# A recurrent layer between attention layers: where its own-token products, roots and softmax scaling are computed

## The chip, the cores and the metric

The kernel runs on one core of a Trainium2 chip. The metric is device time in microseconds (us), lower is better. All data are 32-bit floats. The engines are named as in the profile: PE is TensorE (matmuls; PEld are its weight loads), DVE is VectorE, ACT is ScalarE, POOL is GpSimd, and SP only issues transfers.

## What is computed

Four layers on x (8 sequences, 100 tokens, 512 channels) with a context of 361 tokens: grouped attention, a recurrent layer, a small attention, and a pair of attentions with an MLP. The change lies in the second and third:

```python
# second layer, per head of 16 channels (32 heads), tokens l in order
w = jnp.exp(-jnp.exp(time_decay + jnp.tanh(xw @ decay_w1) @ decay_w2))
r, k, v = xr @ Wr.T, xk @ Wk.T, xv @ Wv.T
g = jax.nn.silu(xg @ Wg.T)
def step(s, inp):
    k_l, v_l, w_l, r_l = inp
    a = k_l[..., :, None] * v_l[..., None, :]
    out = einsum('bhs,bhst->bht', r_l, faaaa * a + s)   # faaaa * a: the token's own part
    return a + w_l[..., None] * s, out
y = (y - mean(y)) * rsqrt(var(y) + 1e-5) * gn_w + gn_b  # mean and variance per head
x = x + (y * g) @ Wo.T
x = x + sigmoid(xr2 @ fWr.T) * (square(relu(xk2 @ fWk.T)) @ fWv.T)   # channel mix
# third layer
probs = softmax((x @ w_q.T) @ (ctx @ w_k.T).T / sqrt(512))
x = x + alpha * ((probs @ (ctx @ w_v.T)) @ w_o.T)
```

The own-token part of `out` is v times the sum over a head's 16 channels of r * faaaa * k.

## The kernel before

The second layer works in four units of two sequences (`UB = 2`, so 200 token columns, `UT`). Channels lie on the 128 partitions in four chunks c, so a tensor of one unit is [128, 4, 200]; w, k and v have an extra leading column per sequence. There are three kinds of work.

**Preparation** (`prescan`, lines 608 to 712), one generator for each unit: normalization, token shift, the mixes w, k, v, r, g, then the projections v, k, r (`through`, line 598: two halves of two chunks, each half in one PSUM bank and then evicted), the decay w (`pw`, lines 694 to 708), and g. v is also written to DRAM with 16 transfers (line 687), and read back spread over partitions (`spread_values`, line 721). It has 21 turns (a `yield` ends a turn).

**The scan loop** (lines 997 to 1043), 64 steps of 16 per unit: one step is one chunk c and one i of four. `to_psum` (730) copies the spread values to PSUM on ACT. `states` (738) multiplies them by k (line 743, DVE), scans over the tokens (line 745, DVE) and multiplies by r (line 751, POOL). `gather_heads` (754) sums on PE, a step later, into the bank `py`. In steps 2 and 10 of a unit, `own_token` (line 760) forms the own-token part of two chunks: r * faaaa * k on DVE from SBUF (line 766, tile `ruk`), a matmul that sums over the head and spreads over the channels of v (line 770, bank `pu`), and the product with v into y (line 771).

**What follows the scan**: `head_norms` (775) for each half of a unit adds `py` to y (779), subtracts the mean (784), squares (786), sums the squares (791), and takes the root (793, ACT) into two of the four row groups of `sd`. `after` (795) inverts the roots (797), spreads them over the channels (803), applies gn_w, gn_b and g (805, 808), projects, and does the channel mix (lines 823 to 844); for units 1 to 3 its last act is `turned_rows` (846), which transposes x and adds the mix on eviction (line 858). `mixing` (871) is the third layer: for unit 0 it turns its own rows and then ends a turn (886 to 888), then queries (890), scores, softmax (898 to 903), and the rest.

**What sets the order.** All PE instructions are issued in program order (`L1_ORDERED`); the other engines' instructions are ordered by the program's scheduler, which uses its own estimates. In each scan step `advance` (line 945) gives every running generator one turn, or more or fewer by its rate: 1.6 for the preparation of unit 1, 1.1 for later ones, 1.0, 1.2, 1.4 and 1.0 for what follows units 0 to 3. The preparation of unit 0 runs ahead of the loop. Whatever is left when the 64 steps are over runs behind the loop, units by turns.

**Buffers.** Nearly all matmul results of this layer use one tag of three PSUM banks (`bank`, line 540). v, k, r, y and w have two buffers each, so unit u + 2 takes those of unit u; `sd` has one. A buffer is given to the next tile when every instruction on the former one is done. The third layer's tiles of units 1 and 3 take buffers of v and k (`pair_of_tiles`, line 867). The mixes of a preparation have five buffers.

Of the kernel before, what the change touches and what calls it, by code (L numbers as in the profile page):

```python
# [10 lines left out]
F32 = mybir.dt.float32  # L11
AF = mybir.ActivationFunctionType
ALU = mybir.AluOpType
# [3 lines left out]
P = 128  # L17
B, L, C, S = 8, 100, 512, 361
# [38 lines left out]
def kernel(ctx: ExitStack, tc: tile.TileContext, d: dict, out: bass.AP):  # L57
    nc = tc.nc
# [11 lines left out]
    eps5 = const.tile([P, 1], F32, tag="eps5", name="eps5")  # L70
# [5 lines left out]
    def col(name, c):  # L76
        at = PV_AT[name] + c
        return pv[:, at : at + 1]
# [123 lines left out]
    with ExitStack() as es:  # L202
# [15 lines left out]
        v = p1.tile([KB, B, 3, 8 * HV + 16], F32, tag="v", name="v")  # L218
# [292 lines left out]
    with ExitStack() as es:  # L511
# [31 lines left out]
        def two(t):  # L543

            return t[:, : 2 * UT].rearrange("p (c t) -> p c t", c=2)
# [4 lines left out]
        def split(t):  # L550
            return t.rearrange("p c (b l) -> p c b l", l=L)
# [46 lines left out]
        def through(w, m, evict_to):  # L598

            for h in range(2):  # L600
                pp = bank("pp")
                for i in range(2):
                    c = 2 * h + i
                    mm_sum(two(pp)[:, i], [(w[:, k, c * P : (c + 1) * P], m[:, k]) for k in range(NC)])
                evict_to(slice(2 * h, 2 * h + 2), two(pp))
                yield

        def prescan(u, out):
# [81 lines left out]
                            )  # L690
            r = pb.tile([P, NC, UT], F32, tag="r", name="r")
            out["r"] = r
            yield from through(wts["r"], mixes["r"], lambda cs, pp: nc.scalar.copy(r[:, cs], pp))
            for h in range(2):
                pw = bank("pw")
                for i in range(2):
                    c = 2 * h + i
                    nc.tensor.matmul(
                        two(pw)[:, i], lhsT=dw2[:, c * P : (c + 1) * P], rhs=dt, start=True, stop=True
                    )  # L700
                for i in range(2):
                    c = 2 * h + i
                    nc.scalar.activation(
                        two(pw)[:, i], two(pw)[:, i], AF.Exp, bias=col("L1_xattn_time_decay", c), scale=1.0
                    )
                nc.scalar.activation(
                    wT[:, 2 * h : 2 * h + 2, :, 1:], split(two(pw)), AF.Exp, scale=-1.0
                )
                yield
            g = pb.tile([P, NC, UT], F32, tag="g", name="g", bufs=2)  # L710
            out["g"] = g
# [45 lines left out]
                    py[32 * q : 32 * q + 32].rearrange("p (b l) -> p b l", l=L), lhsT=gather[:, i], rhs=st[:, q], start=(i == 0), stop=(i == 3)  # L757
                )

        def own_token(u, c):  # L760

            k, r, v, y = (ready[u][j] for j in "krvy")
            pu = bank("pu")
            for i in range(2):
                ruk = pb.tile([P, UT], F32, tag="ruk", name="ruk")
                nc.vector.scalar_tensor_tensor(
                    ruk.rearrange("p (b l) -> p b l", l=L), r[:, c + i].rearrange("p (b l) -> p b l", l=L),
                    col("L1_xattn_faaaa", c + i), k[:, c + i, :, 1:], ALU.mult, ALU.mult,
                )
                nc.tensor.matmul(two(pu)[:, i], lhsT=heads[:, 0], rhs=ruk, start=True, stop=True)  # L770
            nc.vector.tensor_tensor(
                split(y[:, c : c + 2]), split(two(pu)), v[:, c : c + 2, :, 1:], ALU.mult
            )

        def head_norms(u, c, py):

            y, sd = ready[u]["y"], ready[u]["sd"]
            cs = slice(c, c + 2)
            nc.vector.tensor_tensor(y[:, cs], two(py), y[:, cs], ALU.add)
            yield  # L780
            pg = bank("pg")
            for i in range(2):
                nc.tensor.matmul(two(pg)[:, i], lhsT=heads[:, 1], rhs=y[:, c + i], start=True, stop=True)
            nc.vector.tensor_tensor(y[:, cs], y[:, cs], two(pg), ALU.subtract)
            sq = pb.tile([P, 2, UT], F32, tag="sq", name="sq", bufs=1)
            nc.scalar.activation(sq, y[:, cs], AF.Square)
            yield
            pvar = bank("pvar")
            for i in range(2):
                at = 32 * (c + i)  # L790
                nc.tensor.matmul(pvar[at : at + 32, :UT], lhsT=pick8, rhs=sq[:, i], start=True, stop=True)
            rows = slice(32 * c, 32 * c + 64)
            nc.scalar.activation(sd[rows], pvar[rows, :UT], AF.Sqrt, bias=eps5[rows], scale=1.0)

        def after(u, turned=None, rest=None):
            y, g, sd = (ready[u][j] for j in ("y", "g", "sd"))
            nc.vector.reciprocal(sd, sd)
            yield
            for c0 in (0, 2):
                pair = [bank("rs") for _ in range(2)]  # L800
                for c, rs in zip((c0, c0 + 1), pair):
                    qs = slice(32 * c, 32 * c + 32)
                    nc.tensor.matmul(rs[:, :UT], lhsT=heads[qs, 2], rhs=sd[qs], start=True, stop=True)
                for c, rs in zip((c0, c0 + 1), pair):
                    nc.vector.scalar_tensor_tensor(
                        y[:, c], y[:, c], col("L1_xattn_gn_w", c), rs[:, :UT], ALU.mult, ALU.mult
                    )
                    nc.vector.scalar_tensor_tensor(
                        y[:, c], y[:, c], col("L1_xattn_gn_b", c), g[:, c], ALU.add, ALU.mult
                    )  # L810
                yield
            bs = range(u * UB, (u + 1) * UB)
            for i, b in enumerate(bs):
                po = bank("po")
                mm_sum(po[:L, :], [(y[:, c, i * L : (i + 1) * L], wo1[:, c, :]) for c in range(NC)])
                nc.vector.tensor_tensor(x[b], po[:L, :], x[b], ALU.add)
                stats(pb, b)
                yield
            cols = slice(u * UB, (u + 1) * UB)
            nc.scalar.activation(rstd[:, cols], mv[:, cols, 1], AF.Sqrt, bias=eps5[:L], scale=1.0)  # L820
            nc.vector.reciprocal(rstd[:, cols], rstd[:, cols])
            yield
            got = []
            yield from normed(u, mv, rstd, "L1_xattn_ln2_w", "L1_xattn_ln2_b", got, 0)
            xu = got[0]
            sx = shifted(u, xu, 0)
            yield

            xk, xr, kk = y, sx, xu
            mixed_by(xk, sx, xu, "L1_xattn_fmaa_k")  # L830
            mixed_by(xr, sx, xu, "L1_xattn_fmaa_r")
            yield
            yield from through(wfk, xk, lambda cs, pp: nc.scalar.activation(kk[:, cs], pp, AF.Relu))
            nc.gpsimd.tensor_tensor(kk, kk, kk, ALU.mult)

            yield from through(wfr, xr, lambda cs, pp: nc.scalar.activation(xk[:, cs], pp, AF.Sigmoid))
            yield from through(wfv, kk, lambda cs, pp: nc.vector.tensor_tensor(xk[:, cs], pp, xk[:, cs], ALU.mult))
            if turned is not None:
                tiles = turned()
                tiles.extend(pair_of_tiles((("r", L), ("w", L1)) if u % 2 == 0 else (("v", L1), ("k", L1))))  # L840
                turned_rows(bs, tiles[0], xk)
                rest.append(lambda: added_rows(bs, xk))
            else:
                added_rows(bs, xk)
# [26 lines left out]
        def mixing(u, pool, wqk, wvo, xT, qk, rest=()):  # L871
# [13 lines left out]
                loaded.append((cx, cr))  # L885
            if not rest:
                turned_rows(bs, xT)
                yield
            scale = 1.0 / float(np.sqrt(np.float32(C)))
            yield from through(wqk, xT, lambda cs, pp: nc.scalar.activation(qk[:, cs], pp, AF.Copy, scale=scale))  # L890
            for add in rest:
# [2 lines left out]
            for i, b in enumerate(bs):  # L894
                sc = bank("sc")
                mm_sum(sc[:L, :S], [(qk[:, c, i * L : (i + 1) * L], loaded[i][0][:, c, :]) for c in range(NC)])
                nm = pool.tile([L, 1], F32, tag="nm", name="nm")
                nc.vector.tensor_reduce(nm, sc[:L, :S], AX.X, ALU.max, negate=True)
                pr = pool.tile([L, S], F32, tag="pr", name="pr")
                ss = pool.tile([L, 1], F32, tag="ss", name="ss")  # L900
                nc.scalar.activation(pr, sc[:L, :S], AF.Exp, bias=nm, scale=1.0, accum_out=ss)
                nc.vector.reciprocal(ss, ss)
                nc.vector.tensor_scalar(pr, pr, ss, None, ALU.mult)
                probs.append(pr)
                yield

# [78 lines left out]
        with tc.manual_schedule(engines=L1_ORDERED):  # L985
# [11 lines left out]
            for n in range(NU * STEPS + 1):  # L997
                u, c, i = n // STEPS, n % STEPS // 4, n % 4
                if u < NU:
# [16 lines left out]
                    if n + 1 < NU * STEPS:  # L1016
                        m = n + 1
                        a = to_psum(m // STEPS, m % STEPS // 4, m % 4, va.pop(0))
                    if n % (STEPS // 2) == 2:
                        own_token(u, c)  # L1020
                advance()
                if late is not None:
                    lu, lc, li, lst = late
# [758 lines left out]
```

## Time and profile before

| What | us |
| --- | --- |
| Runs shown: median (lowest to highest of 3) | 2722.99 (2721.82 to 2725.64) |
| Profiled execution: span from the first to the last instruction | 2722.8 |
| PE busy in the span | 2609.8 |
| Scan loop of the second layer, from about 365 to 745 | 380 |
| the rest of the second and third layers behind the loop, to about 829 | 84 |
| DVE busy in the stretch from 365 to 745 | 282.9 |
| ACT busy in the same stretch | 167.9 |

The profile gives no time around its span; span and median agree within 0.2 us. The page has, besides busy times, a line for each engine with the busy share in 40 slices of 68 us each. Other views of the same trace group the instructions by line, engine and tile; list who waited for whom (an engine's idle time ahead of an instruction is put down to the instruction that ended it); follow back the chain of waits; and show the instructions in order of time, where a bracket behind an instruction holds the idle time ahead of it and who ended it. Two PE instructions in the trace make one matmul of 32-bit floats. A duration in the groups and rows is in ns, a start in us from the span's beginning.

### The profile page before, as it was taken

How to read it: one execution, taken by the hardware profiler on the slowest of the kernel's cores; microseconds unless marked ns; L12 is line 12 of the kernel's file. 1: busy time of each engine (PE TensorE's matmuls, PEld its weight loads, DVE VectorE, ACT ScalarE, POOL GpSimd, SP SyncE). 2: the span in 40 equal slices, each digit the busy share in tenths (PEclk: the TensorE clock that was granted, in tenths of full speed). 3: DMA queues.
4: the chain of work that ended last, by engine and by line, in shares of the span. 5: the costliest groups of instructions: out<-in, count | busy, mean ns of one | idle time of the engine just before them, and what ended most of it. 6: DMA issues, size and time to landing. Idle time of an engine off the chain costs nothing.

```text
span 2722.8 us, 39771 instructions
## 1 busy us (share of the span) xinstructions
PE 2609.8 (96%) x14100; PEld 2059.3 (76%) x14100; DVE 1601.2 (59%) x3987; ACT 939.2 (34%) x2143; POOL 1042.7 (38%) x1362
## 2 busy tenths in 40 slices
PE   8999889898989999999999999999999999999999
PEld 5666466676666888877789878788877788887688
DVE  4888366877524556556556556565555655654733
ACT  5777334543321333320333320243331143331211
POOL 2000144433204345455345446344446434535201
PEclk9999888999999999999999999999999999999999
DMA  7432334354214100046200034400015510005400
GB/s 230 119 104 75 115 116 124 92 145 122 81 39 151 55 23 23 4 126 169 80 23 23 1 85 145 136 16 31 12 35 151 150 43 23 23 7 168 152 13 13
DMA packets 149679, 220.58 MB, mean 81 GB/s; under 512 B 45302, under 2 KB 78646, under 8 KB 149226
## 3 DMA queue, kind: packets, MB, share of 16 engines
q1 hardware_dynamic: 149482, 218.05, 27.3%
q8 instruction: 112, 1.84, 0.3%
q14 instruction: 85, 0.70, 0.1%
HBM read 207.48 MB, written 10.53 MB: 80 GB/s over the span
## 4 chain that ended last, share of the span: by engine, by line
PE 67%; POOL 4%; DVE 3%; DMA 2%; ACT 1%; issue 1%; SPq 0%; DVEq 0%; POOLq 0%; ACTq 0%
PE pz L97 16%; PE sl L97 9%; PE pk L1175 6%; PE su L97 6%; PE pq L97 5%; PE pa L97 5%; PE po L1439 5%; PE pp L97 3%; PE pu L97 3%; PE pt L1363 2%; PE pl L97 2%; PE pl L1262 1%; DMA xin<-xd 1%; PE sc L1401 1%; PE sc L97 1%
## 5 line engine op out<-in xcount | busy, mean ns | idle before, releaser
L97 PE MATMUL pz<-at,cr 121*128 121x256 f32 (+1 forms) x960 | 255.9, 378 | 0.0
L751 POOL TENSOR_TENSOR st<-st,r 128x800 f32<-128x800 f32 x64 | 111.9, 1749 | 232.9 <-DVE st L745 198.9
L1336 DVE TENSOR_TENSOR qz<-pz,qz 128x512 f32<-128x512 f32 x192 | 131.9, 687 | 114.0 <-PE pz L97 105.8
L97 PEld LDWEIGHTS pz<-at,cr 121*128 121x128 f32 (+1 forms) x960 | 177.2, 189 | 20.8
L1175 PE MATMUL pk<-q,wb 128*128 128x400 f32 x512 | 190.2, 501 | 0.0
L97 PE MATMUL pa<-qz,wa 128*128 128x400 f32 x512 | 178.7, 500 | 0.8 <-DVE aT L1479 0.8
L97 PE MATMUL sl<-ts,ss 128*128 128x181 f32 x768 | 156.7, 326 | 3.8 <-POOL ts L1231 0.5
L97 PE MATMUL pz<-at,cs 121*128 121x256 f32 (+1 forms) x576 | 149.7, 380 | 0.0
L1248 POOL TENSOR_TENSOR ss<-qz 128x256 f32<-128x256 f32 x96 | 69.8, 727 | 203.3 <-PE su L97 115.0
L97 PEld LDWEIGHTS pa<-qz,wa 128*128 128x128 f32 x512 | 95.7, 190 | 65.9 <-DVE aT L1479 2.3
L1382 ACT ACTIVATE pr<-su,nm 128x362 f32<-128x362 f32 x96 | 54.1, 564 | 265.0 <-DVE nm L1378 264.9
L1366 ACT COPY at<-pt 121x384 f32<-121x384 f32 x192 | 84.2, 480 | 159.9 <-PE pt L1363 95.6
L1091 ACT COPY qz<-pk 128x400 f32<-128x400 f32 x128 | 63.0, 492 | 214.8 <-PE pk L1175 214.8
L97 PEld LDWEIGHTS sl<-ts,ss 128*128 128x128 f32 x768 | 118.4, 190 | 21.9 <-issue 7.1
L1175 PEld LDWEIGHTS pk<-q,wb 128*128 128x128 f32 x512 | 93.7, 190 | 45.7 <-ACT qz L1091 3.7
L745 DVE TENSOR_TENSOR_SCAN st<-wd,a 128x808 f32<-128x808 f32 x64 | 117.0, 1828 | 16.1 <-PE py L756 14.3
L350 PEld LDWEIGHTS pt<-ident,pr 115*121 115x121 f32 (+1 forms) x672 | 83.2, 185 | 56.5 <-ACT at L230 29.2
L1385 ACT ACTIVATE pr<-pr,ss 128x362 f32<-128x362 f32 x200 | 113.1, 594 | 29.1 <-DVE ss L1383 28.9
L1448 DVE TENSOR_TENSOR acc<-po,acc 128x400 f32<-128x400 f32 x196 | 111.4, 572 | 15.1 <-PE po L1439 0.5
L342 ACT ACTIVATE pr<-pr,nm 115x361 f32<-115x361 f32 (+1 forms) x224 | 115.2, 592 | 10.4 <-DVE nm L338 10.4
L97 PEld LDWEIGHTS pz<-at,cs 121*128 121x128 f32 (+1 forms) x576 | 104.4, 189 | 13.7 <-issue 1.8
L338 DVE CUSTOM_DVE_ANT_0 pr<-sc,mask 115x361 f32<-115x361 f32 (+1 forms) x224 | 106.0, 530 | 11.0 <-PE sc L326 10.4
(383 smaller groups left out, 6180.0 us busy)
## 6 DMA issues: line engine op xcount, KB each, us to landing
va<-vd SPq DMA_DIRECT2D x64, 404.0 KB
wa<-in_L_xattn_wq SPq DMA_DIRECT2D x64, 256.0 KB
wb<-in_L_xattn_wk SPq DMA_DIRECT2D x64, 256.0 KB
wa<-in_L_xattn_wv SPq DMA_DIRECT2D x64, 256.0 KB
wb<-in_L_xattn_wo SPq DMA_DIRECT2D x64, 256.0 KB
u<-pd SPq DMA_DIRECT2D x64, 200.0 KB
cr<-in_ctxR SPq DMA_DIRECT2D x16, 726.0 KB
cx<-in_ctxT SPq DMA_DIRECT2D x16, 722.0 KB
```

The costliest lines, as they stand in the source:

```text
L97: nc.tensor.matmul(dst, lhsT=lt, rhs=r, start=(i == 0), stop=(i == len(pairs) - 1))
L338: nc.vector.tensor_tensor_reduce(out=pr[:n], in0=sc[:n, :S], in1=mk[t][:n], scale=-1.0, scalar=FLT_MAX, op0=ALU.add, op1=ALU.min, accum_ou ...
L342: nc.scalar.activation(pr[:n], pr[:n], AF.Exp, bias=nm[:n], scale=-1.0)
L350: nc.tensor.transpose(pt[:KB, k * n : (k + 1) * n], pr[:n, lo : lo + KB], ident[:n, :n])
L745: nc.vector.tensor_tensor_scan(st.rearrange("p q b l -> p (q b l)"), wd.rearrange("p q t -> p (q t)"), a, 0.0, ALU.mult, ALU.add,)
L751: nc.gpsimd.tensor_tensor(st, st, rc.unsqueeze(1).to_broadcast([P, 4, UB, L]), ALU.mult)
L1175: nc.tensor.matmul(pk[:, :HT], lhsT=wk[:, c * P : (c + 1) * P], rhs=q, start=True, stop=True)
L1336: nc.vector.tensor_tensor(dst, pz, other, ALU.add)
L1366: nc.scalar.copy(at, pt[:KB, : 3 * TR].rearrange("p (k r) -> p k r", r=TR))
L1385: nc.scalar.activation(pr[:, : S + 1], pr[:, : S + 1], AF.Copy, scale=ss)
L1439: nc.tensor.matmul(po[:, c], lhsT=left[k][:, c * P : (c + 1) * P], rhs=right[k], start=True, stop=True)
L1448: nc.vector.tensor_tensor(acc[k], po, acc[k], ALU.add)
```

## The change

Four edits, all in the second and third layers:

1. `own_token` moves from the scan loop to the preparation. When a half of r arrives in PSUM, ACT copies it to SBUF as before, and DVE forms r * faaaa * k from the same PSUM bank; the result goes to the mix tile of k, whose projection is done. Behind each half of the decay w, the matmul over heads and the product with v follow. The product is written over v itself, in place, and no longer to y; `head_norms` then adds `py` and v into y.
2. `head_norms` copies the sums of squares to `sd`, and `after` takes one root for all four row groups of a unit, ahead of the reciprocal.
3. In the softmax of the third layer, the scaling by the reciprocal of the sum moves from DVE to ACT.
4. `mixing` ends a turn ahead of its queries for every unit, not only for unit 0: so between the turned rows and the first matmul that reads them lies one turn.

```diff
             r = pb.tile([P, NC, UT], F32, tag="r", name="r")
             out["r"] = r
-            yield from through(wts["r"], mixes["r"], lambda cs, pp: nc.scalar.copy(r[:, cs], pp))
+            ruk = mixes["k"]
+
+            def received(cs, pp):
+                nc.scalar.copy(r[:, cs], pp)
+                for i, c in enumerate(range(cs.start, cs.stop)):
+                    nc.vector.scalar_tensor_tensor(
+                        ruk[:, c].rearrange("p (b l) -> p b l", l=L), split(pp)[:, i],
+                        col("L1_xattn_faaaa", c), out["k"][:, c, :, 1:], ALU.mult, ALU.mult,
+                    )
+
+            yield from through(wts["r"], mixes["r"], received)
             for h in range(2):
                 pw = bank("pw")
...
                 nc.scalar.activation(
                     wT[:, 2 * h : 2 * h + 2, :, 1:], split(two(pw)), AF.Exp, scale=-1.0
                 )
+                own_token(out["v"], ruk, 2 * h)
                 yield
...
-        def own_token(u, c):
-
-            k, r, v, y = (ready[u][j] for j in "krvy")
+        def own_token(v, ruk, c):
+
             pu = bank("pu")
             for i in range(2):
-                ruk = pb.tile([P, UT], F32, tag="ruk", name="ruk")
-                nc.vector.scalar_tensor_tensor(
-                    ruk.rearrange("p (b l) -> p b l", l=L), r[:, c + i].rearrange("p (b l) -> p b l", l=L),
-                    col("L1_xattn_faaaa", c + i), k[:, c + i, :, 1:], ALU.mult, ALU.mult,
-                )
-                nc.tensor.matmul(two(pu)[:, i], lhsT=heads[:, 0], rhs=ruk, start=True, stop=True)
-            nc.vector.tensor_tensor(
-                split(y[:, c : c + 2]), split(two(pu)), v[:, c : c + 2, :, 1:], ALU.mult
-            )
+                nc.tensor.matmul(two(pu)[:, i], lhsT=heads[:, 0], rhs=ruk[:, c + i], start=True, stop=True)
+            own = v[:, c : c + 2, :, 1:]
+            nc.vector.tensor_tensor(own, split(two(pu)), own, ALU.mult)
 
         def head_norms(u, c, py):
...
-            nc.vector.tensor_tensor(y[:, cs], two(py), y[:, cs], ALU.add)
+            nc.vector.tensor_tensor(split(y[:, cs]), split(two(py)), ready[u]["v"][:, cs, :, 1:], ALU.add)
             yield
...
-            nc.scalar.activation(sd[rows], pvar[rows, :UT], AF.Sqrt, bias=eps5[rows], scale=1.0)
+            nc.scalar.copy(sd[rows], pvar[rows, :UT])
 
         def after(u, turned=None, rest=None):
             y, g, sd = (ready[u][j] for j in ("y", "g", "sd"))
+            nc.scalar.activation(sd, sd, AF.Sqrt, bias=eps5, scale=1.0)
             nc.vector.reciprocal(sd, sd)
             yield
...
             if not rest:
                 turned_rows(bs, xT)
-                yield
+            yield
...
                 nc.vector.reciprocal(ss, ss)
-                nc.vector.tensor_scalar(pr, pr, ss, None, ALU.mult)
+                nc.scalar.activation(pr, pr, AF.Copy, scale=ss)
...
-                    if n % (STEPS // 2) == 2:
-                        own_token(u, c)
```

## The prediction

> **What bounds the kernel now.** First the page's busy line and slices: TensorE is 96% busy over the span, and its gaps lie in slices 5 to 12. There nothing else is near full, so TensorE and what holds it up set the time.
>
> ```profile
> PE 2609.8 (96%) x14100; PEld 2059.3 (76%) x14100; DVE 1601.2 (59%) x3987; ACT 939.2 (34%) x2143; POOL 1042.7 (38%) x1362
> PE   8999889898989999999999999999999999999999
> DVE  4888366877524556556556556565555655654733
> ```
>
> Then the second layer by stretches: the scan loop, and the tail behind the last scan step. Columns: window, length, busy time (and count) of PE, PEld, DVE, ACT, POOL, granted clock, DMA.
>
> ```profile
> 365.00:745.00 380.00, 334.51 (x1973) 244.97 (x1974) 282.92 (x365) 167.94 (x318) 153.16 (x94) 0.93 0.37 108
> 745.00:829.00 84.00, 72.01 (x356) 52.29 (x351) 22.63 (x53) 16.72 (x34) 3.20 (x3) 0.94 0.14 43
> ```
>
> The loop leaves TensorE idle for 380 - 334.5 = 45.5 us; the change removes no matmul, so this idle time is all that it can win (the tail holds little that it touches). Next, who ends those gaps (total us, times, longest):
>
> ```profile
> PE pm L634 <- DVE mix L642: 4.3, 3, 1.8
> PE pp L97 <- DVE v L858: 4.1, 1, 4.1
> PE pvar L791 <- ACT fo L196: 1.7, 1, 1.7
> PE tp L910 <- DVE pr L903: 1.5, 1, 1.5
> PE sc L97 <- DVE y L771: 1.5, 1, 1.5
> PE pp L97 <- DVE y L771: 1.1, 1, 1.1
> ```
>
> The reader sees many small stalls, released by VectorE and ScalarE: late evictions, not one bound.
>
> **Part 1, own-token products.** The instructions' durations (min/median/max ns; the last row has busy us and mean ns):
>
> ```profile
> L766 DVE SCALAR_TENSOR_TENSOR ruk<-r,pv,k x16: 394/1367/1912, 353.7 to 641.3; 128x200 f32<-128x200 f32 x16
> L642 DVE SCALAR_TENSOR_TENSOR mix<-pm,pv,sx x48: 390/410/427, 379.5 to 541.8; 128x200 f32<-128x200 f32 x48
> L903 DVE TENSOR_SCALAR pr<-pr,ss x8: 404/410/1931, 657.9 to 814.7; 100x361 f32<-100x361 f32 x8
> L793 ACT ACT_TABLE_LOAD x7 | 9.0, 1283 | 0.1
> ```
>
> The same instruction on the same shape takes up to 1.91 us from SBUF while GpSimd multiplies, and never above 0.43 us where one operand comes from PSUM. The change reads r from PSUM, so VectorE loses 16 x 1.165 = 18.6 us (18.2 listed) and gains 16 x 0.41 = 6.6: **11.6 us less**. The 16 matmuls and the eight 0.55 us products stay and only move. The sum with y (L779) has one PSUM operand before and after.
>
> Two places show what the long ones delay. At 418 us, two take 3.25 us; the state chain behind them is late, and TensorE then waits 1.7 us (pvar) and 1.8 us (g, for wT) at 428 to 431. I count 1.7. At 507 us two more stand 3.3 us before the small `nb` that the next rows need; the transposes and pvar then lose 0.6 + 0.3 + 1.1 = 2.0. At 377 us 2.2 us stand before a mix eviction: 1.8. Together 5.5.
>
> The second gain is a PSUM bank. Today the product is written into y, two buffers by turns, so unit 2 waits until unit 0 has had y transposed:
>
> ```profile
> 548.85 0.94 PE L770 MATMUL pu<-ruk,heads 128*128 128x200 f32 x4
> 565.36 0.64 PE L864 MATMUL pr<-ident,y 128*100 128x128 f32 x4 [2.02 <-DVE x L865]
> 566.53 0.51 DVE L771 TENSOR_TENSOR y<-pu,v 128x400 f32<-128x400 f32 x1
> ```
>
> One of three banks is held for 17.7 us (and for 10 us from 638.75, ending at 648.7 behind y's other buffer). Written in place into v, nothing waits for y: the stalls of 2.0, 1.1 and 1.5 us are then gone: 4.6.
>
> What it adds. The in-place write must follow the 16 transfers that read v. Unit 1's are issued from 398.0 to 408.1 and its decay products come at 424.5, so they are over; unit 0's end their issue at 353.1, some 4 us before the product, and what stands behind it on VectorE (the first a x k at 361.26) waits for the spread values anyway. v lives longer: unit 2's v eviction at 469.3 now follows unit 0's sum at 461.9, unit 3's at 555 that at 542. Only the turned tile of unit 1 (v's buffer, L858 at 632.5) falls behind the sum now at 633.5: 0.6 us, covered by the added turn. The r banks are now released by VectorE behind its scans of 1.83 us, and each decay bank is followed by one more: 12 banks in the loop. The nearest row is the mix eviction, also two VectorE instructions on a bank: 4.3 us of stall over 24 banks, 0.18 each: 12 x 0.18 = **2.2 us lost** (bounds: nothing, and a scan each, 22 us). In unit 0's preparation 1.4 us of matmul move ahead of the loop; scan and gather leave TensorE idle 7 us between 363 and 373, so 0 to 1 us, I take 0.5. **Part 1: 5.5 + 4.6 - 2.7 = 7.4 us.**
>
> **Part 2, one root per unit.** Eight roots (0.423 us, 64 rows) become eight copies (nearest 0.331, `dt`, 64 rows) and four roots of 128 rows (0.42): 3.4 against 2.6 + 1.7. Of the table loads those between silu and tanh (516.98, and tanh's own at 519.45) and those at 431.3 and 607.2 go: four, 4 x 1.28 = 5.1 us of ScalarE. On the path only the pair at 517: TensorE waits 1.5 us at 521.1 for `ta`. **1.5.** In the tail the root is some 0.4 us later; its reciprocal ends at 757.1, its matmul starts at 764.05, so it is covered. [...] The trace shows the next activation 0.02 us behind the 1.28 us load (516.98, then 518.28), so the sum goes by 1.28.
>
> **Part 3, softmax on ScalarE.** VectorE loses 7.7 us (eight, mean 0.96; three of the four in the loop are stretched to 1.8 to 1.93). ScalarE gains eight of about 0.60, the row of the same scaling in the fourth layer (580/597/615). TensorE's wait of 1.5 us at 659.96 shrinks by 1.93 - 0.6, and a x k behind it comes 1.9 us earlier: I count **1.5**. Added wait: ScalarE now stands for the reciprocal, behind it the next spread-value copy, for which a x k and the scan wait. It idles 3.7 and 7.8 us there, so nothing in the loop (at worst a scan of 1.83 each, four times); in the tail, where the scaling is alone at 0.41, 0.3 lost. [...]
>
> **Part 4, the turn.** At 628.99 TensorE stops for 4.1 us: it needs the turned tile that VectorE evicts behind a x k. With a turn between, the next in its order is the gather, whose state GpSimd finishes at 631.77: 2.8 us of stall stay, 1.3 are won, and 0.5 at 734.8. **1.8.** The loads of this step are issued ahead of the turn, so no queue is passed. Unit 1 ends a turn later, 14 us before the loop's end; unit 2's rest moves among work that keeps TensorE full to 773.
>
> **Sum.** Stalls touched: 5.5 + 4.6 + 1.5 + 1.5 + 1.8 = 14.9. They are not all won: VectorE (283 of 380 us) or GpSimd is late next. I take three quarters, 11.2, since VectorE's own load falls too (11.6 + 7.7 = 19.3 us); less 2.2 + 0.5 + 0.3 = 3.0 that is 8.2. A second way: in the chain of waits from 640 to 742 us VectorE has 29.6 of 102 us, 29%; 19.3 x 0.29 = 5.6, + 4.6 (banks) + 1.5 (table) - 3.0 = 8.7. The fourth layer behind it is TensorE at 99%, and simply moves. The profiled span is 2722.8 us, and the median of the runs 2722.99, so the difference carries over: 2723 - 8 = **2715 us**. If all 19.3 us counted, -19.3 - 1.5 + 3.0 = -17.8: **2705**. Own range 2705 to 2719.
>
> **Rivals.** *The stalls change places*: only the banks and the table count, 4.6 + 1.5 - 3.0 = 3.1: 2720, no change that can be told (a measurement of this kernel tells about 0.2%, 5.4 us). For it: VectorE waits 45.9 us for ScalarE's copies and 14.3 us for TensorE in the loop, so it is itself often not the last. Against: the stalls named have its long instructions right before them. That the product does not get faster from PSUM falls in here: 11.6 x 0.29 = 3.4 us fewer, 2718; no PSUM row speaks for it. *The banks become the bound*: r twice, then decay, product, decay, product ask for six of three banks in a row, and each is released by VectorE behind a scan or by ScalarE behind a table load and three exponentials (today's waits for wT: 2.3 us). At 1.5 us for each of 12 banks it is 18 us against 11.2 - 0.5 - 0.3 = 10.4 won: **2731**, slower; it decides from about 0.9 us a bank. Against it stands the 0.18 of the mix banks.
>
> **How the numbers follow.** Forecast 0.60, places change 0.22, banks 0.18. The range runs from 2705 to 2729: it takes in both forecast and first rival and the nearer half of the second. Faster by over 0.2% (below 2717.5) 0.60, within 0.22, slower 0.18.
>
> **What would show it.** Right: the products at 0.41 with no long one; no pu held over 2 us; VectorE's busy time in the second layer down 19 us; about four fewer table loads; TensorE's idle time in the loop down to 34 to 38 us. Wrong: new waits of TensorE for `ruk`, `wT` or `v` around r and the decays, a scan loop that is no shorter, or ScalarE idle on `ss` with a x k late behind it.

## The result, and the profile after

The changed kernel takes **2735.5 us** (median of 8 runs, 2730.4 to 2740.9); the kernel before, in the runs beside it, 2724.3. Ratio **1.0034 [1.0022, 1.0046]**: slower by 0.34%, where 0.3% faster was forecast. All times below are ratios to runs of the kernel before on the same chip, with a 95% interval.

The profiled execution of after (span 2728.2 us, its run 2730.4, the lowest of the eight). First the page's busy line and slices, then the two stretches (columns as before: window, length, PE, PEld, DVE, ACT, POOL, granted clock, DMA).

```profile
PE 2624.4 (96%) x14100; PEld 2068.7 (76%) x14100; DVE 1586.3 (58%) x3979; ACT 938.7 (34%) x2151; POOL 1040.8 (38%) x1362
PE   8999889898989999999999999999999999999999
DVE  4788366876524556556556556565555655654733
```

```profile
365.00:745.00 380.00, 342.59 (x2020) 249.14 (x2020) 270.34 (x364) 169.62 (x331) 153.08 (x94) 0.92 0.39 113
745.00:829.00 84.00, 72.20 (x315) 55.42 (x315) 17.64 (x40) 16.49 (x32) 3.20 (x3) 0.80 0.08 23
```

The forecast idle time is there: TensorE idles 380 - 342.6 = 37.4 us in the first stretch, against 45.5, and 34 to 38 were foretold. Over the span its idle time falls from 113.0 to 103.8 us. But the same 14100 instructions now take 2624.4 us instead of 2609.8. The column that tells why is the clock: **0.80 in the tail, where it was 0.94**. The work did not grow; it ran slower.

The waits of TensorE from 350 to 745 us (total us, times, longest):

```profile
PE pt L97 <- DVE mix L596: 5.3, 1, 5.3
PE pm L634 <- DVE mix L642: 4.5, 3, 1.8
PE pp L97 <- issue: 4.3, 1, 4.3
PE px L857 <- DVE y L842: 2.7, 1, 2.7
...
PE px L857 <- DVE v L863: 2.3, 1, 2.3
...
PE tp L915 <- ACT pr L908: 1.8, 1, 1.8
...
PE pp L97 <- DVE v L777: 1.3, 1, 1.3
```

Gone are the waits for y (L771) and for x (L865); those for wT fall from 2.7 to 1.0 us. New are two longer ones at the loop's start (`pt` 5.3 instead of 3.1, and the g projection, "issue", 4.3 instead of 0.6), two for the turned tile's bank (`px`), and one for the softmax at 742.94 us.

The instructions that the change touches, min/median/max ns:

```profile
L698 DVE SCALAR_TENSOR_TENSOR mix<-pp,pv,k x16: 416/418/427, 352.7 to 583.9; 128x200 f32<-128x200 f32 x16
...
L908 ACT ACTIVATE pr<-pr,ss x8: 583/590/598, 654.4 to 814.3; 100x361 f32<-100x361 f32 x8
```

Both durations are those of the forecast (0.41 and 0.60).

**Where the time came from.** From the last scan to the first instruction of the fourth layer the profile has 730.7 to 829.6 = 98.9 us before, 723.8 to 835.8 = 112.0 us after. The tail's softmax, in order of time, first before, then after (start, duration; the bracket is TensorE's idle time and who ended it):

```profile
742.33 2.60 PE L97 MATMUL sc<-cx,w 128*100 128x361 f32 x8
745.34 2.68 PE L97 MATMUL sc<-cx,w 128*100 128x361 f32 x8
747.85 0.43 PE L910 MATMUL tp<-ident,pr 100*128 100x100 f32 x3
```

```profile
736.11 5.03 PE L97 MATMUL sc<-cx,w 128*100 128x361 f32 x16
742.94 0.48 PE L915 MATMUL tp<-ident,pr 100*128 100x100 f32 x3 [1.80 <-ACT pr L908]
743.26 0.86 PE L787 MATMUL pg<-y,heads 128*128 128x200 f32 x4
743.96 4.96 PE L97 MATMUL pz<-probT,cr 128*128 128x100 f32 x24
```

Before, unit 2's two scorings had other work between them (a gather at 744.86), and no wait followed. After, the added turn puts them back to back, and ScalarE does exponential, exponential, scaling, scaling: TensorE stands 1.80 us, and again at 814.47 for unit 3 (1.23 us before). The 24 `pz` instructions then take 4.96 us; before, unit 2's took 2.97. Cut into the stretches in which the granted clock changes (3.41 us each), with the clock behind the five engines:

```profile
740.94:744.35 3.41, 1.61 (x12) 1.35 (x12) 1.32 (x5) 1.86 (x5) 0.00 (x0) 1.00 1.00 328
744.35:747.77 3.42, 3.42 (x18) 3.42 (x18) 0.38 (x1) 0.54 (x1) 0.00 (x0) 0.50 0.11 36
747.77:751.18 3.41, 2.90 (x14) 1.89 (x14) 0.37 (x1) 1.88 (x3) 0.00 (x0) 0.50 0.33 95
751.18:754.59 3.41, 3.30 (x15) 3.05 (x16) 1.40 (x1) 0.93 (x3) 0.00 (x0) 0.50 0.32 121
754.59:758.01 3.42, 3.42 (x13) 2.57 (x13) 0.00 (x0) 0.49 (x1) 0.00 (x0) 0.50 0.21 8
758.01:761.42 3.41, 3.41 (x11) 1.14 (x9) 0.49 (x1) 0.00 (x0) 0.00 (x0) 1.00 0.59 208
812.62:816.03 3.41, 1.15 (x9) 0.94 (x9) 1.14 (x4) 1.87 (x5) 0.00 (x0) 1.00 0.00 0
816.03:819.45 3.42, 3.42 (x18) 3.42 (x18) 0.00 (x0) 0.00 (x0) 0.00 (x0) 0.50 0.00 0
```

A window in which TensorE was busy 1.61 of 3.41 us is followed by four at half clock, and so is the one at 812.62 with 1.15 us.

### The profile page after: what moved, and what is told of

It is laid out like the page before. It is cut to its first block, busy times and chain, and to the rows that moved or that the text cites. A ratio compares the mean times of both kernels' runs of the same rounds, so it can differ in the third digit from the quotient of the medians.

```text
span 2728.2 us, 39804 instructions
## 1 busy us (share of the span) xinstructions
PE 2624.4 (96%) x14100; PEld 2068.7 (76%) x14100; DVE 1586.3 (58%) x3979; ACT 938.7 (34%) x2151; POOL 1040.8 (38%) x1362
## 4 chain that ended last, share of the span: by engine, by line
PE 79%; DVE 6%; POOL 4%; ACT 4%; DMA 4%; issue 2%; SPq 1%; DVEq 0%; POOLq 0%; ACTq 0%
PE pz L97 17%; PE sl L97 9%; PE pk L1178 6%; PE su L97 6%; PE pq L97 5%; PE pa L97 5%; PE po L1442 5%; PE pp L97 5%; PE pu L97 3%; PE pt L1366 2%; PE pl L97 2%; PE pt L350 2%; PE po L97 2%; DVE st L756 2%; ACT pr L342 1%
## 5 line engine op out<-in xcount | busy, mean ns | idle before, releaser
L97 PEld LDWEIGHTS pz<-at,cs 121*128 121x128 f32 (+1 forms) x576 | 104.4, 189 | 13.7 <-issue 1.8
```

The source lines that it names most:

```text
L97: nc.tensor.matmul(dst, lhsT=lt, rhs=r, start=(i == 0), stop=(i == len(pairs) - 1))
```

## The experiments

Theory A: a pause of TensorE lowers its granted clock for what follows, and the tail's softmax pauses are what made the change slower. Theory B: scaling on ScalarE costs in itself, or the denser loop lowers the clock anyway. Later: C, the own-token products stand at the wrong place in the preparation; D, there was nothing to win by part 1; E, any shift of the tail does it.

All runs in one table. Each kernel has 8 to 12 runs (e16 five), against 8 of before for after and 29 to 35 for the others. e1 to e4, e5 to e8, e9 to e12 and e13 to e16 were run on four chips, so kernels of different groups are compared by their ratios to before. "Clock" is the mean granted clock of the timed runs (before: 0.980 to 0.982 in the four groups of runs). The last three columns are of one profiled execution: the last scan's start, the time from there to the fourth layer's first instruction, and the half-clock time from the last scan's start to 850 us (so pauses at the fourth layer's start are in it).

| Kernel | Ratio to before | Clock | Last scan | Tail, us | Half clock |
| --- | --- | --- | --- | --- | --- |
| before | 1 | 0.981 | 730.7 | 98.9 | 10.2 |
| after | 1.0034 [1.0022, 1.0046] | 0.978 | 723.8 | 112.0 | 34.1 |
| e1 after, softmax on VectorE | 0.9994 [0.9984, 1.0005] | 0.980 | 732.2 | 100.7 | 20.5 |
| e2 after, no turn | 1.0022 [1.0012, 1.0031] | 0.979 | 737.3 | 104.0 | 26.1 |
| e3 part 3 alone | 1.0009 [0.9998, 1.0020] | 0.980 | 728.4 | 103.9 | 27.3 |
| e4 part 1 alone | 1.0013 [1.0003, 1.0024] | 0.981 | 735.0 | 102.7 | 23.9 |
| e5 after, softmax split | 0.9991 [0.9979, 1.0004] | 0.981 | 727.1 | 100.8 | 13.7 |
| e6 after, pauses filled | 0.9973 [0.9961, 0.9985] | 0.982 | 726.9 | 101.6 | 10.2 |
| e7 after, products last | 0.9992 [0.9979, 1.0004] | 0.980 | 727.8 | 101.8 | 10.2 |
| e8 split, products last | 0.9977 [0.9967, 0.9988] | 0.980 | 728.9 | 100.8 | 17.1 |
| e9 part 2 alone | 0.9999 [0.9988, 1.0009] | 0.981 | 729.8 | 102.7 | 23.9 |
| e10 part 4 alone | 1.0003 [0.9990, 1.0015] | 0.981 | 734.4 | 100.4 | 17.1 |
| e11 part 1 alone, products last | 1.0004 [0.9992, 1.0017] | 0.979 | 735.3 | 103.1 | 27.3 |
| e12 products last, pauses filled | 0.9991 [0.9981, 1.0001] | 0.981 | 728.1 | 101.7 | 10.2 |
| e13 after, same work elsewhere | 1.0030 [1.0015, 1.0044] | 0.978 | 732.1 | 112.9 | 32.4 |
| e14 after, first pause filled | 1.0018 [1.0008, 1.0028] | 0.978 | 734.8 | 106.3 | 26.1 |
| e15 e6, normalization filled too | 0.9989 [0.9978, 0.9999] | 0.982 | 733.7 | 98.8 | 6.8 |
| e16 split, last, filled | 0.9961 [0.9949, 0.9974] | 0.983 | 725.2 | 97.8 | 6.8 |

The loop's end is not to be read from one execution: up to the tail, after, e6, e13, e14 and e15 are the same program, and their last scans start at 723.8, 726.9, 732.1, 734.8 and 733.7.

**e1, part 3 undone in the changed kernel.**

```diff
-                nc.scalar.activation(pr, pr, AF.Copy, scale=ss)
+                nc.vector.tensor_scalar(pr, pr, ss, None, ALU.mult)
```

> The changed kernel, with the softmax scaling back on VectorE (part 3 undone alone). Theory A (in the tail, the scaling on ScalarE stretches TensorE's wait ahead of the transposes from 1.2 to 1.8 us, and a window with that wait in it puts the granted clock to half for some 14 us, twice, about 6 us each): the wait is back at 1.2 us, the half-clock stretches at about 744 and 816 us are gone, 2735 - 12 = 2723 us or less. Theory B (the clock falls because the scan loop leaves TensorE fewer gaps and more load; the softmax is innocent): 2732 to 2736 us, the half-clock stretches of the tail stay.

0.9994: the 0.40% between it and after (10.9 us) hang on this one line. In its profile both waits are 1.23 us, and no half-clock stretch begins at either.

**e2, part 4 undone in the changed kernel.**

```diff
                 turned_rows(bs, xT)
-            yield
+                yield
```

> The changed kernel without the added turn (part 4 undone alone). Theory A: unit 2's scores stand again with the last gather between them, so the first of the two waits is short and its half-clock stretch (at 744 us) goes; the second, at 815 us, stays: 2735 - 6 = 2729 us, and the 4 us wait for the turned tile at about 630 us may come back (+1 to 3). Theory B: no change, 2733 to 2737.

1.0022. The stretch at 744 is gone; unit 3's pause still trips the clock (half clock follows). TensorE's idle time from 365 to 745 us is 41.4 us, against 35.4 to 38.6 in five executions with the turn, and the loop ends later than in any of them: the turn seems to win there, but this is one execution.

**e3 and e4, parts 3 and 1 alone in the kernel before.**

> The kernel before with the softmax scaling on ScalarE (part 3 alone). Theory A: the wait of 1.2 us at 814 us becomes 1.8 us and trips the clock: 2724 + 6 = 2730 us; less if the loop wins 1 to 2 us. Theory B: 2721 to 2725, no half-clock stretch at the softmax.

> The kernel before with the own-token products formed in the preparation (part 1 alone). Theory A: the scan loop ends about 5 to 7 us earlier, the tail is that of before: 2717 to 2719 us. Theory B: the shorter loop is paid back by a lower clock: 2723 to 2732 us.

Part 3 alone gives 1.0009, with a half-clock stretch at 814.7 behind a pause of 1.80 us. This decides nothing: the time lies between the theories (A's 2730 us is a ratio of 1.0022, B's upper end 1.0003), and e4, e9 and e11 have such a stretch behind unit 3's old pause of 1.23 us. Part 1 alone gives 1.0013, and not the gain forecast. Its idle time from 365 to 745 us is 44.0 us, hardly below 45.5. TensorE's waits from 360 to 740 us:

```profile
PE pp L97 <- DVE v L862: 5.9, 1, 5.9
PE pn L577 <- ACT xhat L564: 5.5, 1, 5.5
PE pt L97 <- DVE mix L596: 5.2, 1, 5.2
PE pp L97 <- issue: 4.7, 1, 4.7
```

All four are waits that before has too, at 4.1, 3.0, 3.1 and (the g projection) 0.6 us: 10.5 us longer together. At the loop's start the order of ScalarE explains it: a spread-value copy that waits for its transfer until 361.54 now stands ahead of the decay's exponentials, so a bank for the g projection comes free only at 363.55, and the first scan starts at 364.55 instead of 362.37. The other profiles bear this out: it starts at 362.3 to 365.0 in the nine with part 1 at this place (mean 363.9), at 361.1 to 362.8 in the four without part 1 (mean 362.0), and at 360.2 to 363.4 in the five of e7, e8, e11, e12 and e16, where the products stand last (mean 361.8).

**e5 and e6: scaling on VectorE in the tail alone, or the pause filled.**

```diff
-                nc.scalar.activation(pr, pr, AF.Copy, scale=ss)
+                if u < 2:
+                    nc.scalar.activation(pr, pr, AF.Copy, scale=ss)
+                else:
+                    nc.vector.tensor_scalar(pr, pr, ss, None, ALU.mult)
```

> The changed kernel, but units 2 and 3 (whose softmax lies in the tail behind the scan loop) scale on VectorE as before; units 0 and 1, inside the loop, keep ScalarE. Theory A (the pause of TensorE at the tail's softmax, 1.8 us instead of 1.2, is what makes the granted clock fall to half, and ScalarE's scaling in the loop is a gain): the loop ends at about 724 as in the changed kernel, the half-clock stretches at 744 and 816 are gone, the fourth layer begins at about 825, and the time is 2717 to 2722 (ratio to before 0.996 to 0.999). Theory B (any scaling on ScalarE costs, by the spread-value copies that wait behind it): it stays between the changed kernel and the one with all scaling on VectorE, 2727 to 2735.

```diff
+            if u > 1:
+                idle = ps.tile([P, 2, 512], F32, tag="a", name="idle")
+                for j in range(6):
+                    nc.tensor.matmul(idle[:, 0, :P], lhsT=ident, rhs=ident, start=True, stop=True)
             for i, b in enumerate(bs):
                 pt = bank("tp")
```

> The changed kernel with six added matmuls of 128 columns (identity by identity, into a PSUM bank that nobody reads) ahead of the transposes of the probabilities of units 2 and 3: about 1.5 us of work that fills TensorE's pause at the softmax. All scaling stays on ScalarE. Theory A: no half-clock stretch starts at 744 or 816, the fourth layer begins 8 to 12 us earlier than at 838, the time is 2722 to 2728 although work was added (ratio to before 0.998 to 1.001). Theory B (the clock has nothing to do with the pause): the added work costs 0 to 3 us, 2735 to 2739.

e5 0.9991, on the edge of theory A's range (0.996 to 0.999), and e6 **0.9973**: 0.61% below after (16.6 us), though 3.0 us of useless work were added. In order of time, and by the clock's windows:

```profile
739.12 5.03 PE L97 MATMUL sc<-cx,w 128*100 128x361 f32 x16
743.99 1.50 PE L915 MATMUL idle<-ident 128*128 128x128 f32 x12
745.95 0.49 PE L919 MATMUL tp<-ident,pr 100*128 100x100 f32 x3 [0.46 <-ACT pr L908]
```

```profile
744.22:747.63 3.41, 2.95 (x25) 2.70 (x24) 1.56 (x5) 1.87 (x5) 0.00 (x0) 1.00 0.97 318
812.49:815.90 3.41, 2.49 (x21) 2.14 (x21) 0.53 (x2) 1.56 (x5) 0.00 (x0) 1.00 0.00 0
815.90:819.31 3.41, 2.95 (x28) 2.78 (x27) 0.37 (x1) 0.73 (x2) 0.00 (x0) 1.00 0.00 0
```

The wait shrinks from 1.80 to 0.46 us, no window with a pause in it is below 2.49 us busy, and the clock stays full. Theory A's time is beaten, B's 2735 to 2739 excluded.

**e7, e8: the products behind g,** in the changed kernel, and with e5's split.

```diff
                 nc.scalar.activation(
                     wT[:, 2 * h : 2 * h + 2, :, 1:], split(two(pw)), AF.Exp, scale=-1.0
                 )
-                own_token(out["v"], ruk, 2 * h)
                 yield
...
             yield from through(wts["g"], mg, lambda cs, pp: nc.scalar.activation(g[:, cs], pp, AF.Silu))
+            for h in range(2):
+                own_token(out["v"], ruk, 2 * h)
+                yield
```

> The changed kernel, but the matmuls and products of the own token stand behind the projection of g, as the last two turns of the preparation, instead of between the halves of the decay. Theory C (at the loop's start the decay's exponentials and the g projection were held up by the four banks pw, pu, pw, pu and by the order that ScalarE got from it: g 4.7 us of pause, first scan 2.2 us later): first scan back at about 362.4, g's pause under 1 us, and the time 2 to 4 us below the changed kernel, 2731 to 2734. Theory D (the late start is due to VectorE's hold on the r banks): first scan stays at 363.5 or later, time as the changed kernel, 2734 to 2737.

> Both edits at once: units 2 and 3 scale on VectorE, and the own-token matmuls and products stand behind g. Theories A and C: 2714 to 2719, faster than both kernels (ratio to before 0.995 to 0.998). Theory A without C: 2717 to 2722. Theory B: 2727 or more.

e7 0.9992, more than either theory gave (in this expectation D blames VectorE's hold on r's banks). The first scan is back at 362.6, g waits 0.8 us and `pt` 2.7 again, as C has it. But the profile also shows luck: the same two pauses of 1.80 us did not trip; a window's edge cuts each, and no window with a part of one is busy for less than 1.99 us:

```profile
742.07:745.49 3.42, 3.04 (x10) 1.33 (x9) 0.88 (x2) 0.65 (x2) 0.00 (x0) 1.00 0.45 119
745.49:748.90 3.41, 1.99 (x16) 1.93 (x17) 1.36 (x5) 2.03 (x6) 0.00 (x0) 1.00 0.94 315
748.90:752.31 3.41, 2.90 (x25) 2.35 (x25) 0.37 (x1) 1.83 (x4) 0.00 (x0) 1.00 0.15 29
810.34:813.75 3.41, 2.35 (x8) 1.00 (x6) 1.09 (x3) 1.11 (x3) 0.00 (x0) 1.00 0.00 0
813.75:817.17 3.42, 2.22 (x18) 2.06 (x19) 0.53 (x2) 1.41 (x5) 0.00 (x0) 1.00 0.00 0
```

e8, 0.9977, is faster than both kernels, within the 0.995 to 0.998 expected.

**e9 to e12.** Parts 2 and 4 alone; part 1 alone with the products last; e7 with e6's fill.

> The kernel before with part 2 alone: copies of the sums of squares and one root per unit. The prediction's theory: 1.5 us won, ratio 0.9994. Rival: the table loads lie beside TensorE's work and the root comes later, 1.000 to 1.001. Both within 0.1% of before; four fewer table loads by either.

> The kernel before with part 4 alone: a turn ahead of the queries of every unit. The prediction's theory: 1.8 us won, ratio 0.9993. Rival (the turn moves the scoring of unit 2 in the tail so that both scorings come back to back, and TensorE then stands for a whole softmax, which may put the clock at half): 1.000 to 1.003; the tail then has two waits for pr instead of one.

> The kernel before with part 1 alone, but the own-token matmuls and products behind the projection of g. Theory C (part 1's gain on VectorE is real, and its place between the halves of the decay ate it): first scan at or before 362.6, ratio 0.996 to 0.999. Theory D (VectorE's load did not set the loop's time, so there is nothing to win): 1.000 to 1.002, as with the products between the decays (1.0013).

> The changed kernel with both mends: own-token products behind g, and six added matmuls in TensorE's pause at the softmax of units 2 and 3. If the two mends add up (pause 0.6%, place 0.2 to 0.4%): ratio to before 0.993 to 0.996. If they are the same gain seen twice (both only remove half-clock stretches in the tail): 0.997 to 0.998.

0.9999 and 1.0003: neither part moves the time alone, within 0.13%. e11's 1.0004 is theory D's: with the products last (first scan 363.4 in its profile, where 362.6 was expected) part 1 still wins nothing that can be told; its idle time from 365 to 745 us is 45.4. e12, 0.9991, is a miss: no better than e7. The mean clocks, 0.980 in e7 and 0.981 in e12, fit this: 0.001 of the span is some 2.7 us (an estimate), and the fill adds 3.0 us of work. Why e7's open pauses cost less than those of after stays open. So the fill seemed to do much in one kernel and nothing in the other, which called for a control.

**e13 to e16: the control, one pause alone, another place, all mends.** e13 puts e6's six matmuls ahead of the scoring, where TensorE has work; e14 fills for `u == 2` only; e15 is e6 with 12 such matmuls ahead of unit 3's second normalization transposes and 14 ahead of its channel mix; e16 joins e8, e15 and a fill of four.

> Control: the changed kernel with the same six added matmuls for units 2 and 3, but ahead of their scoring, where TensorE has work anyway, and not in the pause behind it. Theory A (the filled pause counts, not the added work): the waits of 1.8 us for pr stay, the mean clock stays near 0.978, and the 3.0 us of work are paid: ratio to before 1.003 to 1.005. Rival E (any shift of the tail against the rest does it, or the chip did): as with the pause filled, 0.997 to 0.999.

> The changed kernel with the fill for unit 2 alone (the pause at about 742); unit 3's pause at about 814 stays. Theory A: about half of the way from 1.0034 to 0.9973, 0.999 to 1.002, and a half-clock stretch behind 814 in most executions. Rival E: 0.997 to 0.998 or above 1.003.

> The changed kernel with the softmax pauses filled and, for unit 3, the two pauses of its second normalization as well (3.3 us ahead of the transposes and 3.7 us ahead of the channel mix, 12 and 14 matmuls of 128 columns). The chain through these pauses is not shortened, and 0 to 1 us is lost where the fill ends late. Theory A: the half-clock stretch of 10.2 us from about 776, which every kernel so far shows, goes, and with it 3 to 5 us: ratio to before 0.995 to 0.997, at least 0.001 below the softmax fill alone (0.9973). Rival E: 0.997 to 1.000.

> All mends at once: units 2 and 3 scale on VectorE, own-token products behind g, the tail's softmax pauses (1.2 us) filled with four matmuls, the normalization pauses of unit 3 with 12 and 14. Theory A: the split with products last (0.9977) less 3 to 5 us: 0.995 to 0.997, faster than both kernels. Rival E: 0.997 to 0.999.

The control gives **1.0030** with the same added work that gave 0.9973 in the pause. In its profile both pauses stand open, and the second is followed by four windows at half clock. The first is not, though its window is busy for 1.62 us only; the half clock comes two windows later, behind one with 1.98:

```profile
749.30:752.72 3.42, 1.62 (x7) 0.66 (x6) 0.77 (x3) 1.64 (x6) 0.00 (x0) 1.00 0.92 246
752.72:756.13 3.41, 3.41 (x30) 3.35 (x30) 0.94 (x2) 1.05 (x3) 0.00 (x0) 1.00 0.52 187
756.13:759.54 3.41, 1.98 (x15) 1.26 (x15) 0.80 (x2) 2.80 (x5) 0.00 (x0) 1.00 0.58 188
759.54:762.96 3.42, 3.42 (x17) 3.42 (x18) 0.97 (x1) 0.00 (x0) 0.00 (x0) 0.50 0.08 29
820.98:824.40 3.42, 1.62 (x7) 0.65 (x5) 0.77 (x3) 1.62 (x4) 0.00 (x0) 1.00 0.00 0
824.40:827.81 3.41, 2.95 (x15) 2.92 (x14) 0.37 (x1) 0.24 (x1) 0.00 (x0) 0.50 0.00 0
```

e14 lies between, 1.0018. E falls for the changed kernel: the filled pause counts, not the work nor the shift. The 18 profiles together say how often the tail's softmax pauses trip the clock at the next edge of a window: six of nine pauses of 1.80 us, three of twelve of 1.23 us (unit 3's in e4, e9 and e11), none of nine filled ones (0.34 to 0.46 us left). So half clock follows the pause of before (1.23 us) too in some executions, though not in its own profile. e15 removes the stretch that starts between 773 and 784 us in all earlier profiles, as foretold, but its 0.9989 misses theory A's 0.995 to 0.997 and is not below e6's; why is open. e16 does it all, and is the fastest: **0.9961 [0.9949, 0.9974]**. The same normalization pause, first in before, then filled in e16:

```profile
776.00:786.00 10.00, 5.84 (x21) 5.45 (x22) 2.79 (x8) 2.83 (x6) 1.68 (x2) 0.51 0.01 2
```

```profile
772.00:782.00 10.00, 8.79 (x63) 8.30 (x64) 2.79 (x8) 3.23 (x7) 1.68 (x2) 1.00 0.00 0
```

## Why the prediction was wrong

- **The step that failed is in part 3:** "in the tail, where the scaling is alone at 0.41, 0.3 lost". As a delay of the chain it is about that (a wait of 1.80 instead of 1.23 us). What it costs is the clock behind it: 10.9 us by e1, 11.7 by e5 (0.43%), and 16.6 by e6, which also shortens the pause itself. Part 4 is its partner: the turn took the cover off unit 2's softmax (no wait before, 1.80 us after), where the prediction had unit 2's rest "among work that keeps TensorE full to 773". Under it lies an assumption that was never stated: that a matmul takes the same time after the change. "This idle time is all that it can win" holds; it is not all that can be lost, since a pause of 1.80 us here also slowed the work after it (24 `pz` instructions took 4.96 us behind it, 2.97 before). The clock column stood in the views I read, 0.94 in the tail, and I did not use it.
- **The sum of stalls.** Between forecast and result lie 0.63%; the softmax explains 0.40 to 0.43. With the tail's scaling back on VectorE e5 is at -0.09% [-0.21, +0.04], so the forecast -0.29% is missed there too. The idle time fell to 37.4 us, and in the other four executions of the same loop to 35.4 to 38.6: as forecast, with all parts together. The loop's end did not follow: 723.8 to 734.8, mean 730.3, against 730.7 before and 729.8 in e9. The time at half clock from the first to the last scan is 60.0 to 76.9 us in these five, 54.6 before and 61.4 in e9. That fits idle time turned into slower work here too, but it is not shown: e10, without part 1, has 68.3, and which of the loop's pauses do it was not tried. With the tail's pauses filled, e6 lands at -0.27%, the size of the forecast (-0.29%), but e15 at -0.11%: that the sum was right is not shown.
- **Part 1.** The durations held, VectorE's busy time in the two stretches fell by 17.6 us (19 foretold), the waits for y went, and the in-place write cost nothing that shows. But alone it won nothing: the stalls change places, the first rival, with four waits 10.5 us longer. "0 to 1 us, I take 0.5" for the loop's start was mis-sized: the first scan is 1.9 us later on the mean of the profiles, and g waits 3.6 to 4.7 us. Of the 1.8 us at 377 nothing went: `pm` waits 4.5 us instead of 4.3.
- **Part 2.** Right: there are 39 table loads instead of 43, and in e9 ScalarE sheds 4.4 us and `ta` costs TensorE 0.4 instead of 1.9 us (in e3, without part 2, too). Its 1.5 us are within what 0.9999 allows.
- **Part 4.** Alone it takes 1.9 us off the loop's idle time (43.6 us in e10), the size forecast; in the changed kernel 41.4 without it (e2) stand against 35.4 to 38.6. The loop's end does not show it: 734.4 in e10, 730.7 before. At the place named, where before waits 4.1 us, after waits 2.7 and 2.3, and e2 5.4. In the tail it uncovers the softmax.
- **The rivals.** "The banks become the bound" has the sign and 2731, but its mechanism shows at one place only: at the loop's start g waits 4.3 us, 3.7 more than before, for a bank that ScalarE's exponentials release. The other waits for the products' banks are 1.3 + 0.7 = 2.0 us, for 12 banks 0.17 each, as forecast: 5.7 in all, of the rival's 18. None of the rivals had the clock.

## What to carry to other kernels

Where TensorE sets the time, read the granted clock by stage beside the busy time, and look at what a move leaves TensorE without work for: here two pauses that grew to 1.80 us cost 10.9 (e1) to 11.7 us (e5), with what stood behind them at half clock. A fill of useless matmuls in such a pause is a cheap test (e6: 0.9973, where after has 1.0034), with the same matmuls where there is no pause as its control (e13: 1.0030), and may stay as a mend; but it did not pay everywhere (e12 0.9991 against e7 0.9992, e15 0.9989 against e6 0.9973). And look for an edit that puts two like steps back to back: here the added turn took the cover off unit 2's softmax (no wait before, 1.80 us after).

## What the runs showed of the hardware

In every profile all changes of the granted clock lie on one grid of 3.413 us (after: from 744.35 to 829.69 us are 25 steps of it), whose place against the kernel differs from execution to execution (a half-clock stretch starts at 776.27 us in before and at 778.49 in after, 0.65 of a step apart). Cut along that grid, ten profiles (before, after, e1 to e8; 300 to 2700 us) give, for windows at full clock, how many were followed by half clock:

| TensorE busy in the window | Windows | Followed by half clock |
| --- | --- | --- |
| under 30% | 51 | 51 |
| 30 to 50% | 58 | 49 |
| 50 to 60% | 57 | 26 |
| 60 to 70% | 72 | 28 |
| 70 to 85% | 133 | 9 |
| 85 to 95% | 201 | 3 |
| 95% and more | 6135 | 0 |

Back to full clock it went behind 149 of 193 windows with 95% or more, 16 of 48 with 85 to 95%, and 1 of 62 below. So in these runs it matters where the grid cuts a pause of 1.80 us: after's two left windows with 1.61 and 1.15 us busy, and both tripped; e7's two, each cut by an edge, left 1.99 us and more, and neither did. That is not all: e13's first left 1.62 us and did not trip at the next edge. A cut that differs from execution to execution fits the spread of the times: over the 97 runs of before in e1 to e12, time and clock have a correlation of -0.78. Why some half-clock stretches go on for three or four windows though TensorE is busy (after, 816.03 to 829.69 us: 13.20 of 13.66 us) is open.
